# Two sequences per product in a fused linear-attention and channel-mix kernel

## The chip, the cores and the metric

The kernel runs on one core of a Trainium2 chip. A core has a matrix engine (TensorE, "PE" in the profile, its weight loads "PEld"), a vector engine (VectorE, "DVE"), a scalar engine (ScalarE, "ACT"), GpSimd ("POOL") and a queue engine (SyncE, "SP") that issues nearly all transfers. Work is done on 128 partitions; TensorE writes to PSUM, which has eight banks of 128 x 512 float32 numbers, and all else lies in SBUF or in device memory. The metric is the time on the device in microseconds.

## The reference

The input is `x`, 16 sequences of 1024 positions and 512 channels, float32. With 16 heads of 32 channels:

```python
qkv = x @ Wqkv.T + bqkv
q, k = rmsnorm(q, gq), rmsnorm(k, gk)
qf, kf = relu(rope(q)), relu(rope(k))
vk  = einsum('bhlp,bhld->bhpd', vpad, kf)      # vpad: v and a column of ones
res = einsum('bhpd,bhld->bhlp', vk, qf)
attn = res[..., :-1] / (res[..., -1:] + 1e-6)
x = layernorm(x + rmsnorm(attn @ Wout.T + bout, gout))
# then a channel mix with a shift by one position:
#   out = sigmoid(xr @ W_r.T) * (relu(xk @ W_k.T)**2 @ W_v.T)
x = layernorm(x + out)
```

Attention has no softmax, so all of a sequence's keys and values enter through one 32 x 32 matrix per head (`vk`) and one sum of keys per head.

## The kernel before

**Numbers in two parts.** A product keeps float32 precision by splitting each operand into a high part (rounded to the type float32r) and a low part (what is left). It is made as high x high + high x low + low x high. A split is a copy on ScalarE for the high part and a subtraction on VectorE for the low part.

**Tiles and slots.** `x` is cut into 128 tiles of 128 positions; tile `i` belongs to sequence `b = i // 8`. In the first stage, the function `slot(i)` takes tile `i`: it loads `x` both as it is (`xn`) and transposed (`xt`), projects `q` and `k` (`proj`, 12 products each of 512 columns), applies the rotation (`rope`), stores `q` in device memory for later, and adds to the sequence's `x^T k` (`add_kx`, 12 products into four PSUM banks of their own, `pskx`). GpSimd adds up the keys (`acc`). Values are never computed: since `v = x Wv^T + bv`, the matrix `v^T k` is `Wv (x^T k) + bv (sum of k)^T`.

**Closing a sequence.** In the slots after a sequence's last tile:

- `finish_a(b)` splits `x^T k` out of the four banks into high and low parts side by side (`kx`).
- `finish_s(b)` splits the key sums, adds them over the partitions with a product by ones (`psks`), copies the result to `ksv` and stores one row of it in device memory (`ks_d`).
- `finish_b(b)` makes `v^T k` for four groups of four heads (128 channels each). For each group and each of four chunks of the contraction it issues one product of 256 columns (high weight by the high and low parts of `kx`) and one of 128 columns (low weight by the high part). Two groups share one bank (`pskv`). VectorE adds the bias part, adds the two halves, masks out what lies between different heads and splits the result (`kvth`, `kvtl`).
- `finish_c(b, g)` multiplies group `g` by the output weight's rows for these heads (`w_o`, held in SBUF in two parts), splits it and stores it in device memory (`m_d`). One `finish_c` is done in each of four slots.

Later `load_m` reads that matrix back, and `part_q`, `part_qt`, `part_m`, `part_y` turn stored `q` tiles into the attention output, normalize it and add it to `x`. For the first 11 tiles, `part_q` comes in the first stage, one tile every 8 slots from slot 30; eight of them are carried through `part_y` there. After the last slot comes a transition in a fixed order, then the second stage: the channel mix in `NH` steps of four tiles, with the rest of the attention outputs between.

**Order of the work.** The first slots and the transition are in an order written out by hand. In between, the program gives each tile's work in the order of `slot`, and a planner then lays out each engine's queue from a simulated time line: it takes what is ready by its own costs, the earlier in the program first. Each engine runs its own queue strictly in order. `issue_after(load.ins)` only asks that a transfer stand behind that slot's `xt` load in SP's queue. Four PSUM banks are shared by all that is called `bank(...)` in the first stage: the seeds and products of `q` and `k`, and the closing work above. `late_load` and `late_split` bring in the weights of the later stages in set slots, one of four pieces at a time.

Of the kernel before, what the change touches and what calls it, by code (L numbers as in the profile page):

```python
# [15 lines left out]
P = 128  # L16
DIM = 512
# [5 lines left out]
NQ = 3  # L23
FIRST, STEP = 30, 8
NWARM = 8
HT = 512
# [7 lines left out]
def kernel(  # L34
# [275 lines left out]
    with ExitStack() as a_ctx:  # L310
# [41 lines left out]
        w_a = {h: tx.tile([P, NC_, DIM], F32R, name=f"wa_{h}") for h in "hl"}  # L352
        w_o = {h: te.tile([P, NC_, DIM], F32R, name=f"wout_{h}") for h in "hl"}

# [157 lines left out]

        fin, ksv = {}, {}

        def finish_a(b):

            kx = tx.tile([P, NC_, NC_, 2, P], F32R, tag="kx", name=f"kx{b}")
            for c, ps in enumerate(ps_kx.pop(b)):
                S.copy(kx[:, c, :, 0, :], groups(ps))
                V.tensor_sub(kx[:, c, :, 1, :], groups(ps), f32(kx[:, c, :, 0, :]))  # L520
            fin[b] = kx

        def split_keys(b):
            a = acc.pop(b)
            m = te.tile([P, 2, DIM], F32R, tag="m", bufs=2, name=f"ma{b}")
            S.copy(m[:, 0, :], a)
            V.tensor_sub(m[:, 1, :], a, f32(m[:, 0, :]))
            return m

        def finish_s(b, m=None):  # L530

            m = split_keys(b) if m is None else m
            ps = bank(f"psks{b}")
            for n in range(2):
                T.matmul(ps, lhsT=ones, rhs=m[:, n, :], start=(n == 0), stop=(n == 1))
            ksv[b] = tx.tile([P, DIM], F32, tag="ksv", name=f"ksv{b}")
            S.copy(ksv[b], ps)
            ks_d[b] = dram.tile([NC_, P], F32, name=f"ks_d{b}")
            nc.sync.dma_start(out=ks_d[b].rearrange("g p -> (g p)").unsqueeze(0), in_=ksv[b][0:1, :])

        def finish_b(b, places=(None, None)):

            kx, ks = fin.pop(b), ksv.pop(b)
            th = te.tile([P, NC_, P], F32R, tag="kvth", name=f"kvth{b}")
            tl = te.tile([P, NC_, P], F32R, tag="kvtl", name=f"kvtl{b}")
            for g in range(NC_):
# [21 lines left out]
                if g % 2 == 1:  # L568
                    two = slice(g - 1, g + 1)
                    kv = te.tile([P, 2, P], F32, tag="kv", bufs=1, name=f"kv{b}{g}")  # L570
# [11 lines left out]
                    V.tensor_mul(kv, kv, mask.unsqueeze(1).to_broadcast([P, 2, P]))  # L582
                    S.copy(th[:, two, :], kv)
                    V.tensor_sub(tl[:, two, :], kv, f32(th[:, two, :]))
            fin[b] = th, tl

        def finish_c(b, g, place=None):

            th, tl = fin[b]
            if g == 0:  # L590
                m_d[b] = dram.tile([P, 2, NC_, DIM], F32, name=f"m_d{b}")
            ps = bank(f"psm{b}{g}", place)
            for n, (a, r) in enumerate(((th, "h"), (th, "l"), (tl, "h"))):
                T.matmul(ps, lhsT=a[:, g, :], rhs=w_o[r][:, g, :], start=(n == 0), stop=(n == 2))
            m = te.tile([P, 2, DIM], F32R, tag="m", bufs=2, name=f"m{b}{g}")
            S.copy(m[:, 0, :], ps)
            V.tensor_sub(m[:, 1, :], ps, f32(m[:, 0, :]))
            nc.sync.dma_start(out=m_d[b][:, :, g, :], in_=f32(m))

        late = [("a", wqkv[:, :, 2 * DIM : 3 * DIM], c) for c in range(NC_)]  # L600
        late += [("o", wout, c) for c in range(NC_)]
        for n, w in (("k", wk), ("r", w_r), ("v", wv)):
            late += [(n, w, c) for c in range(NC_)]
            w_d[n] = dram.tile([P, NC_, 2, DIM], F32, name=f"w_d{n}")
# [9 lines left out]
        def late_split():  # L614
            _, n, c, st = staged.pop(0)
            if n in "ao":
                to = {"a": w_a, "o": w_o}[n]
                h, l = (to[k][:, c, :] for k in "hl")
            else:
                m = te.tile([P, 2, DIM], F32R, tag="m", bufs=2, name=f"w{n}{c}")  # L620
                h, l = m[:, 0, :], m[:, 1, :]
# [5 lines left out]
            V.tensor_sub(l, st, f32(h))  # L627
            if n not in "ao":
                nc.sync.dma_start(out=w_d[n][:, c, :, :], in_=f32(m))
# [161 lines left out]
        def late_step(i, load):  # L791
# [8 lines left out]

            if late and (3 <= i < 11 or i % 8 in (7, 0, 1) and not 23 <= i <= 26 and i > 14):
                with tc.issue_after(load.ins):
                    late_load(i)


        loads_m = {23 + c: (0, c) for c in range(NC_)}
        loads_m.update({n: (1, c) for c, n in enumerate((95, 96, 97, 103))})

        def slot(i):
# [12 lines left out]
            if b >= 0 and t == 7:  # L822
                finish_s(b)
            if i - 3 >= 0 and (i - 3) % 8 == 7:
                finish_b((i - 3) // 8)
            if i - 11 >= 0 and (i - 11) % 8 < NC_:
                finish_c((i - 11) // 8, (i - 11) % 8)
            add_kx(i - 1)
# [8 lines left out]
            if i + 2 < N:  # L837
                late_step(i, load)
            j, late_by = divmod(i - FIRST, STEP)
            if i in loads_m:  # L840
# [323 lines left out]
```

## Time and profile before

| | |
|---|---|
| median of 3 runs | 2708.42 us (2707.77 to 2710.29) |
| profiled execution | 2708.87 us, of which 2707.1 us is the span from first to last instruction |
| first stage | until about 1200 us |
| TensorE, share of the span | 99%, 12560 products and as many weight loads |
| VectorE, ScalarE, GpSimd | 80%, 70%, 26% |
| DMA | 433 MB, mean 160 GB/s |
| 300 to 900 us: VectorE, ScalarE, GpSimd busy | 483, 377, 140 of 600 us |
| 300 to 900 us: DMA busy share, rate | 0.76, 244 GB/s |
| one sequence of the first stage (8 slots) | 75.4 us |

In a line of the groups the columns are: line of the kernel, engine, operation, names written and read, shapes, count, then total busy time in us and mean length in ns, then the idle time of the engine just before them and what ended it. A line of the time line begins with start and length in us. Lengths of products overlap, since products are pipelined.

### The profile page before, as it was taken

How to read it: one execution, taken by the hardware profiler on the slowest of the kernel's cores; microseconds unless marked ns; L12 is line 12 of the kernel's file. 1: busy time of each engine (PE TensorE's matmuls, PEld its weight loads, DVE VectorE, ACT ScalarE, POOL GpSimd, SP SyncE). 2: the span in 40 equal slices, each digit the busy share in tenths (PEclk: the TensorE clock that was granted, in tenths of full speed). 3: DMA queues.
4: the chain of work that ended last, by engine and by line, in shares of the span. 5: the costliest groups of instructions: out<-in, count | busy, mean ns of one | idle time of the engine just before them, and what ended most of it. 6: DMA issues, size and time to landing. Idle time of an engine off the chain costs nothing.

```text
span 2707.1 us, 40178 instructions
## 1 busy us (share of the span) xinstructions
PE 2688.8 (99%) x12560; PEld 2230.7 (82%) x12560; DVE 2175.3 (80%) x4880; ACT 1883.2 (70%) x3820; POOL 695.6 (26%) x800
## 2 busy tenths in 40 slices
PE   9999999999999999999999999999999999999998
PEld 7888888888888888877888888888888888888887
DVE  8888888877888788776888888788888888888874
ACT  6666666666666556657777777777777777777775
POOL 4222222222222222234222222222222222222221
PEclk9999999999999999999999999999999999999999
DMA  7788888877777778754232332223133222313210
GB/s 248 241 262 267 259 266 260 264 233 232 228 230 231 251 248 255 247 199 145 90 117 63 105 98 86 88 92 117 59 109 94 87 92 92 113 59 111 73 58 33
DMA packets 232015, 433.29 MB, mean 160 GB/s; under 512 B 24676, under 2 KB 24932, under 8 KB 231800
## 3 DMA queue, kind: packets, MB, share of 16 engines
q1 hardware_dynamic: 231508, 430.19, 49.6%
q8 instruction: 99, 1.62, 0.2%
q14 instruction: 116, 0.95, 0.1%
q10 hardware_dynamic: 292, 0.53, 0.1%
HBM read 314.19 MB, written 116.42 MB: 159 GB/s over the span
## 4 chain that ended last, share of the span: by engine, by line
PE 51%; DVE 1%; ACT 0%; issue 0%; POOL 0%; POOLq 0%; ACTq 0%
PE psk L183 12%; PE psv L183 12%; PE psr L183 12%; PE psy L183 11%; PE pst L168 2%; PE psqt L168 2%; ACT x L288 0%; DVE mixr L901 0%; DVE q L240 0%; DVE mixk L901 0%; DVE gate L1042 0%; DVE mrl L917 0%; DVE qtl L252 0%; ACT gate L1030 0%; DVE den L237 0%
## 5 line engine op out<-in xcount | busy, mean ns | idle before, releaser
L183 PE MATMUL psk<-mkh,w_k 128*128 128x512 f32 x1024 | 332.7, 396 | 1.1 <-DVE kx L520 0.7
L183 PE MATMUL psv<-w_v,kah 128*128 128x512 f32 x1024 | 321.6, 395 | 0.6 <-DVE gate L1042 0.3
L183 PE MATMUL psy<-mb,qth 128*128 128x512 f32 x1024 | 320.0, 389 | 0.3 <-ACT qth L251 0.3
L183 PE MATMUL psr<-w_r,mrh 128*128 128x512 f32 x1024 | 318.6, 396 | 0.0
L183 PEld LDWEIGHTS psy<-mb,qth 128*128 128x128 f32 x1024 | 192.0, 188 | 40.5 <-ACT qth L251 0.7
L487 POOL TENSOR_TENSOR acc<-acc,ro 128x512 f32<-128x512 f32 x96 | 155.7, 1622 | 267.9 <-ACT ro L475 211.7
L183 PEld LDWEIGHTS psk<-mkh,w_k 128*128 128x128 f32 x1024 | 191.3, 188 | 40.3 <-DVE kx L520 1.0
L183 PEld LDWEIGHTS psr<-w_r,mrh 128*128 128x128 f32 x1024 | 188.7, 188 | 36.9 <-ACT r L952 0.2
L183 PEld LDWEIGHTS psv<-w_v,kah 128*128 128x128 f32 x1024 | 187.7, 188 | 38.0 <-DVE gate L1042 0.8
L147 POOL TENSOR_TENSOR rstd_all<-ss,mhalf 128x2 f32<-128x2 f32 x128 | 91.5, 715 | 473.8 <-DVE ss L470 459.5
L917 POOL TENSOR_TENSOR mkl<-mixk,mkh 128x512 fp32r<-128x512 f32 x127 | 165.7, 1305 | 182.4 <-ACT mkh L915 178.0
L429 PE MATMUL psq<-wqk_h,xh 128*128 128x512 f32 x512 | 200.5, 392 | 0.8 <-ACT wqk_h L667 0.8
L183 PE MATMUL psv<-w_v,kal 128*128 128x512 f32 x512 | 200.1, 391 | 0.0
L183 PE MATMUL psk<-mkl,w_k 128*128 128x512 f32 x512 | 199.8, 391 | 0.2 <-DVE mkl L917 0.2
L183 PE MATMUL psy<-mb,qtl 128*128 128x512 f32 x512 | 199.6, 390 | 0.0
L429 PE MATMUL psk<-wqk_h,xh 128*128 128x512 f32 x512 | 199.0, 390 | 0.2 <-ACT psk L360 0.2
L429 PE MATMUL psq<-wqk_l,xh 128*128 128x512 f32 x512 | 198.9, 389 | 0.0
L429 PE MATMUL psq<-wqk_h,xl 128*128 128x512 f32 x512 | 198.8, 389 | 0.0
L429 PE MATMUL psk<-wqk_h,xl 128*128 128x512 f32 x512 | 198.8, 389 | 0.0
L429 PE MATMUL psk<-wqk_l,xh 128*128 128x512 f32 x512 | 198.8, 389 | 0.0
L183 PE MATMUL psr<-w_r,mrl 128*128 128x512 f32 x512 | 196.5, 393 | 0.0
L147 POOL TENSOR_TENSOR yrs<-yss,mhalf 128x1 f32<-128x1 f32 x128 | 70.1, 548 | 395.0 <-DVE yss L300 297.7
(193 smaller groups left out, 7169.9 us busy)
## 6 DMA issues: line engine op xcount, KB each, us to landing
tab<-tab_d SPq DMA_DIRECT2D x480, 256.0 KB
xt<-in_xt_dram SPq DMA_DIRECT2D x128, 256.0 KB
xn<-in_x_dram SPq DMA_DIRECT2D x128, 256.0 KB
q_d<-ro SPq DMA_DIRECT2D x128, 256.0 KB
m_d<-m SPq DMA_DIRECT2D x64, 512.0 KB
mb<-m_d SPq DMA_DIRECT2D x64, 512.0 KB
q<-q_d SPq DMA_DIRECT2D x128, 256.0 KB
out_dram<-x SPq DMA_DIRECT2D x128, 256.0 KB
```

Source lines behind the costliest of these rows:

```text
L147: G.tensor_tensor(dst, src, mhalf[:, 0 : src.shape[1]], ALU.pow)
L168: T.matmul(ps[:, n * P : (n + 1) * P], lhsT=b, rhs=ident, is_transpose=True, start=(n == 0), stop=(n == NC_ - 1), skip_group_check=True,)
L183: T.matmul(ps, lhsT=a[u][:, rows], rhs=b[w][:, cols], start=(afresh and c == 0 and k == 0), stop=(c == n - 1 and k == 2), skip_group_check ...
L429: T.matmul(ps, lhsT=a[i][:, c, :], rhs=w_qk[b][:, c, cols], start=(not seeds and n == 0), stop=(seeds and n == 3 * NC_ - 1), skip_group_ch ...
L487: G.tensor_add(acc[b], acc[b], ros[i])
L917: (V if by_v else G).tensor_sub(ml, m, f32(mh))
```

## The change

Sequences 0 to 13 are taken in seven pairs; the last two stay as they were.

- `finish_a` of a paired sequence copies `x^T k` to SBUF in float32 (`kxf`, both sequences in one tile) and splits nothing.
- `split_kx(p, g)` splits one group of heads of both sequences. The two high parts and the two low parts lie side by side in the tile `stage`. It comes in slots u = 0, 2, 4, 6 of the pair, where u counts from slot 18 + 16 p.
- `finish_pair(p, g)` makes `v^T k` of one group for both sequences in slots u = 1, 3, 5, 7: for each chunk one product of 512 columns and one of 256 columns.
- `finish_c` of the two sequences comes in slots u = 2 to 9, one per slot.
- The key sums of a paired sequence are copied into a row of `acc` and stored; `load_ksv` reads those of both sequences back, on all partitions, half of the columns at a time (u = 0 and 4).
- The output weight is no longer held in SBUF. It is split and stored in device memory like the other late weights, and `load_wo` reads one group's rows into one of two buffers (u = 1, 3, 5, 7). For the last two sequences all four groups are loaded, two of them into the tile `stage` (`load_wo_last`).
- The slots in which later weights are loaded change, and so do those of the first sequence's `load_m` (28 to 31 instead of 23 to 26).

```diff
+PAIRS = 7
-        w_o = {h: te.tile([P, NC_, DIM], F32R, name=f"wout_{h}") for h in "hl"}
...
         def finish_a(b):
+            if paired(b):
+                p, s = divmod(b, 2)
+                if s == 0:
+                    kxf[p] = tx.tile([P, 2, NC_, DIM], F32, tag="kx", name=f"kxf{p}")
+                for c, ps in enumerate(ps_kx.pop(b)):
+                    S.copy(kxf[p][:, s, c, :], ps)
+                return
...
+            if paired(b):
+                row = acc.pop(b)[0:1, :]
+                S.copy(row, ps[0:1, :])
...
+        def load_ksv(p, half):
+            ksv[p, half] = tx.tile([P, 2, 2 * P], F32, tag="ksv", name=f"ksv{p}{half}")
+            cols = slice(half * 2 * P, (half + 1) * 2 * P)
+            nc.sync.dma_start(
+                out=ksv[p, half],
+                in_=ks_p[p].rearrange("s g n -> s (g n)")[:, cols].partition_broadcast(P),
+            )
+        def load_wo(g):
+            w_o[g] = te.tile([P, 2, DIM], F32R, tag="wo", bufs=2, name=f"wo{g}")
+            nc.sync.dma_start(out=f32(w_o[g]), in_=w_d["o"][:, g, :, :])
...
+        def split_kx(p, g):
+            st = te.tile([P, NC_, 2, 2, P], F32R, tag="stage", name=f"kx{p}{g}")
+            for s in range(2):
+                a = kxf[p][:, s, :, g * P : (g + 1) * P]
+                S.copy(st[:, :, s, 0, :], a)
+                V.tensor_sub(st[:, :, s, 1, :], a, f32(st[:, :, s, 0, :]))
+            staged_kx[p] = st
...
+        def finish_pair(p, g):
+            st = staged_kx.pop(p)
+            cols = slice(g * P, (g + 1) * P)
+            ps = bank(f"pskv{p}{g}")
+            four = ps.rearrange("p (s two n) -> p s two n", s=2, two=2)
+            for c in range(NC_):
+                T.matmul(ps, lhsT=w_a["h"][:, c, cols],
+                    rhs=st[:, c].rearrange("p s two n -> p (s two n)"), ...)
+                T.matmul(four[:, :, 0, :], lhsT=w_a["l"][:, c, cols],
+                    rhs=st[:, c, :, 0, :], ...)
+            kv = te.tile([P, 2, P], F32, tag="kv", bufs=1, name=f"kv{p}{g}")
+            V.scalar_tensor_tensor(kv,
+                ksv[p, g // 2][:, :, g % 2 * P : (g % 2 + 1) * P],
+                bv[:, g : g + 1], four[:, :, 0, :], ALU.mult, ALU.add)
+            V.tensor_add(kv, kv, four[:, :, 1, :])
+            V.tensor_mul(kv, kv, mask.unsqueeze(1).to_broadcast([P, 2, P]))
+            th, tl = parts(p, g)
+            S.copy(th, kv)
+            V.tensor_sub(tl, kv, f32(th))
...
-            if late and (3 <= i < 11 or i % 8 in (7, 0, 1) and not 23 <= i <= 26 and i > 14):
+            if late and (3 <= i < 11 or i % 16 > 10 and not 27 <= i < 32):
...
-        loads_m = {23 + c: (0, c) for c in range(NC_)}
+        loads_m = {28 + c: (0, c) for c in range(NC_)}
...
-            if i - 3 >= 0 and (i - 3) % 8 == 7:
-                finish_b((i - 3) // 8)
-            if i - 11 >= 0 and (i - 11) % 8 < NC_:
-                finish_c((i - 11) // 8, (i - 11) % 8)
+            p, u = divmod(i - 18, 16)
+            if 0 <= p < PAIRS and u in (0, 2, 4, 6):
+                split_kx(p, u // 2)
+            if 0 <= p < PAIRS and u in (1, 3, 5, 7):
+                finish_pair(p, u // 2)
+            if 0 <= p < PAIRS and 2 <= u < 10:
+                finish_c(2 * p + u % 2, u // 2 - 1)
+            if i == 8 * 2 * PAIRS + 10:
+                finish_b(2 * PAIRS)
+            if 0 <= i - 8 * 2 * PAIRS - 11 < NC_:
+                finish_c(2 * PAIRS, i - 8 * 2 * PAIRS - 11)
...
+            if 0 <= p < PAIRS and u in (0, 1, 3, 4, 5, 7):
+                with tc.issue_after(load.ins):
+                    if u % 4 == 0:
+                        load_ksv(p, u // 4)
+                    else:
+                        load_wo(u // 2)
+            u = i - 8 * 2 * PAIRS - 9
+            if 0 <= u < NC_:
+                with tc.issue_after(load.ins):
+                    (load_wo, load_wo_last)[u % 2]((0, 2, 1, 3)[u])
```

## The prediction

> **What bounds the kernel now.** I read the busy shares first, then the chain that ended last, then TensorE's waits, then the groups of the edited lines, then the time line around one of them. Page, parts 1, 2 and 4:
>
> ```profile
> span 2707.1 us, 40178 instructions
> PE 2688.8 (99%) x12560; PEld 2230.7 (82%) x12560; DVE 2175.3 (80%) x4880; ACT 1883.2 (70%) x3820; POOL 695.6 (26%) x800
> ...
> PEclk9999999999999999999999999999999999999999
> ...
> PE 51%; DVE 1%; ACT 0%; issue 0%; POOL 0%; POOLq 0%; ACTq 0%
> ```
>
> TensorE is never idle and never throttled. Its waits between 100 and 1000 us are none, and between 1000 and 1200 us one of 0.5 us (for `kh`). So the first stage, which the change rewrites, lasts as long as TensorE's instructions do: time taken out of them comes off the end, unless another engine's lateness takes their place.
>
> What an instruction costs is the distance between starts, not the listed length (a busy TensorE is modelled). Time line of TensorE, columns start and length:
>
> ```profile
> 180.61 0.34 PE L552 MATMUL pskv<-kx,wa_h 128*128 128x256 f32 x1
> 180.78 0.23 PE L560 MATMUL pskv<-kx,wa_l 128*128 128x128 f32 x1
> 180.84 0.33 PE L552 MATMUL pskv<-kx,wa_h 128*128 128x256 f32 x1
> ...
> 184.37 0.39 PE L429 MATMUL psq<-wqk_h,xh 128*128 128x512 f32 x1
> 184.59 0.39 PE L429 MATMUL psq<-wqk_l,xh 128*128 128x512 f32 x1
> 184.82 0.39 PE L429 MATMUL psq<-wqk_h,xl 128*128 128x512 f32 x1
> ```
>
> A 512-column step is 0.226 us. A 256-column product and the 128-column one after it take 0.231 together (180.61 to 180.84), though they stream fewer columns than one 512: two weight loads set that, 0.115 each. The transposes, 128 columns each, step at 0.109, the same limit.
>
> **The change part by part.**
>
> *Products.* Per sequence `finish_b` issues 16 pairs of 256 and 128 columns: 16 x 0.231 = 3.70 us, 7.39 for two sequences. `finish_pair` does two in 16 pairs of 512 and 256 columns. The 512 step is 0.226. The trace has no run of 256-column steps under such a partner. Bounds: 0.109 (transpose step, weight load alone) to 0.171 (the longest distance that follows a 256-column start, 180.61 to 180.78). I take 0.115, half the pair above, since half a 512 step is 0.113 too. Then 16 x 0.341 = 5.46; saved 1.93 per pair of sequences, 13.5 us for seven pairs; by the bounds 14.2 and 7.3. The skill's "TensorE: Matmul & The Clock Gate", sections "Back-to-back issue gap" and "LDWEIGHTS", gives columns/2.4 + 2.5 ns and 128/1.2 = 107 ns per load. By it the old pair is 216 ns, the new one 325, and the saving 112 x 107 ns = 12.0. The rows say 231 and 226 where it says 216 and 216, so I use the rows.
>
> *Copies.* For 14 sequences `finish_a` now only copies four banks to float32 on ScalarE (4 x 0.598, row of L519); `split_kx` then copies and subtracts from SBUF, 8 of each per pair. ScalarE gains 56 copies x 0.62 = 35 us, beside a busy share of 59 to 66% in this stage. VectorE's 56 subtractions move from a PSUM source to an SBUF source. Rows:
>
> ```profile
> L520 DVE TENSOR_TENSOR kx<-pskx,kx 128x512 fp32r<-128x512 f32 x64 | 39.8, 681 | 2.4 <-ACT kx L519 2.3
> L348 DVE TENSOR_TENSOR xnl<-xn,xnh 128x512 fp32r<-128x512 f32 x128 | 94.3, 736 | 43.9 <-ACT xnh L347 43.9
> L476 DVE TENSOR_TENSOR kl<-ro,kh 128x512 fp32r<-128x512 f32 x128 | 108.1, 845 | 62.4 <-ACT ro L475 62.4
> ```
>
> From PSUM 681 ns, from SBUF 736 or 845. The skill's "SBUF — State Buffer", section "Who interferes with whom", speaks against this move: a VectorE instruction with two SBUF inputs blocks against a GpSimd instruction that reads SBUF, for all of it. This trace agrees: a `kl` of 1.49 us at 479.35 beside GpSimd's `acc` sum at 479.01 (1.28 us). By the `xnl` row the move costs 56 x 0.055 = 3 us of VectorE; by the rule up to a whole `acc` sum each, 56 x 1.62 = 91, or 13 per pair. GpSimd is busy 23% of the stage and a hit lasts half a sum on average: 0.23 x 0.8 x 56 = 10, or 1.5 per pair, an estimate. I take that. Against it `finish_pair` has four half-width scalar products fewer per pair, 8 x 0.34 against 4 x about 0.45 (between 0.34 and 0.68; nearest the 256-wide rows of 0.41 to 0.44): 0.9 per pair back.
>
> The PSUM banks of `pskx` come free after the copies alone; four subtractions no longer stand before the next sequence's first `add_kx`. TensorE did not wait there, so nothing for this.
>
> *DMA.* Per pair four `load_wo` of 512 KB and two `load_ksv` of 256 KB, all on SP's queue: 2.6 MB in eight slots of about 9.4 us, beside 244 GB/s at a busy share of 0.76 (full rate 320 GB/s by division). That is 35 GB/s more: about 0.87 while it lasts; six issues of 0.32 to 0.5 us per 75 us of SP. Each `wo` half-buffer is freed two slots before its load and read one slot after: hidden. The `ksv` halves land a slot ahead of VectorE: hidden. At the end (slots 121 to 124) a `wo` buffer is freed in the same slot as its reload; a late one holds SP's `xt` and table loads behind it and costs one wait of at most 3 us, which I put at 0.3. The output weight's four stores (512 KB) fall in the first 100 us, as its splits do already; the later weight loads only change slots. The first sequence's `mb` loads move from slots 23 to 26 to slots 28 to 31, the last one slot ahead of its product, with one load a slot as before. If that slot (over 8 us) did not cover the landing (5.6 us from issue to use for `q`), TensorE would wait once, by a few us. I put nothing for these. The sum row is now copied into `acc`, so GpSimd's first `acc` sum waits for that row's store. Before, `ksv` was copied at 468.60 and the sum began at 479.01: 10 us for a 2 KB store; nothing.
>
> *Crowding.* This is what could cost. Before, nearly every slot had one piece of side work; now slots u=0 to 7 of each sixteen have the pair's work too, and u=5, 6, 7 coincide with `part_q`, `part_m`/`part_y` and `finish_a`. VectorE per slot by rows: 6.56 base (`xl`, `xnl`, two ropes, `kl`); split 1.4; pair 1.97; `finish_c` 0.68; `part_q` with `part_qt` 3.6; `part_y` 2.4; `finish_a` 2.7; sums 0.73. The rows' ends overlap: eight slots sum to 69 by them, but the windows show 62.1 and 62.6 of 75.4 us busy, so x 0.89. Densest four slots before (i mod 8 = 7, 0, 1, 2): 40.0 x 0.89 + 3.5 wait for `q` = 39.1, against TensorE's 39.9. After (u = 4 to 7): 42.5 x 0.89 + 3.5 = 41.3 against 41.7. The slack falls from 0.8 to 0.4. How near that is to a stall:
>
> ```profile
> 429.08 0.79 DVE L233 SCALAR_TENSOR_TENSOR pr<-q,ksb 128x512 f32<-128x512 f32 x1 [3.55 <-DMA q<-q_d]
> ...
> 431.25 0.69 DVE L476 TENSOR_TENSOR kl<-ro,kh 128x512 fp32r<-128x512 f32 x1
> ```
>
> `kl` ends at 431.94 and TensorE starts the product that reads it at 433.02: 1.1 us of margin behind a 3.55 us wait for `q`. In other slots this margin is down to 0.05 us (between 940 and 1060 us). So I allow 0.15 us a pair, 1.0 in all.
>
> **Sum.** Span 2707.1, of a profiled execution of 2708.87: -13.5 + 1.0 + 0.3 = -12.2, giving 2694.9 and 2696.7. That execution lies 0.4 us above the median of the runs, 2708.42; from the median 2696.2. I predict 2696.2, faster by 0.45%. A difference under 0.2% (5.4 us) could not be told from none.
>
> **Rivals.** *A: `q` lands late and takes back the gain.* In u=4 `q` shares the queue with half a `ksv` (256 KB) and comes after a `wo` (512 KB): at 320 GB/s 0.8 and 1.6 us more, 2.4 less the margin of 1.1 = 1.3 a pair, 9 us. Time 2704 to 2706, about no change. For: all eleven `part_q` of this stage waited, 37.4 us together. Against: only every second `q` falls in u=4, and it was asked for 5.6 us before.
>
> *B: VectorE becomes the bound in u=0 to 7; slower.* Place: `kl`, or the seeds of `psq`, which wait for a bank that VectorE reads last: five banks' worth of tiles (`psq`, `psk`, `pskv`, `psm`, `psqt` or `psks`) pass through four in u=5 and 7, where four was the most before. For: the `psq` seed after `finish_b` ended at 482.06 with its product at 482.81. Against: `pskv` now holds a bank for 8 products, not 16. If port blocking is nearer the rule (5 us a pair in place of 1.5), the 0.4 slack becomes a lag of 3 us: seven times 3 is 21, time 2717. From a stall of 1.9 us a pair (13.5 / 7) nothing is left of the gain; beyond it the kernel is slower.
>
> *C: the 256 step stays at 0.171.* Saved 7.3: 2702. Against: weight loads alone never step slower than 0.115 in this trace.
>
> **Chances and range.** Forecast (2692 to 2700) 0.60; C and partial stalls (2700 to 2703) 0.10; A and what else ends near no change (2703 to 2714) 0.14; B (over 2714) 0.16. Faster by over 0.2% (under 2703) is the first two, 0.70; same 0.14; slower 0.16. The range for 8 in 10 takes in the first two and most of A and leaves out B: 2692 to 2710.
>
> **What would show it.** Right: products of `finish_pair` at 0.34 per pair of starts; TensorE's instructions 224 fewer each of products and loads; its waits still near none up to 1000 us; the start of the last sequence's products some 13 us earlier. Wrong: waits of TensorE for `kl`, `psq` seeds or `pskv`, once per sixteen slots; `kx` subtractions well over 0.74; the wait of `pr` for `q` over 3.6. A wrong sum would come from the order that the planner writes for each engine, which the edits redraw throughout the stage and which this trace can't show.

## The result and the profile after

The changed kernel takes 2741.66 us, the median of 4 runs (2739.19 to 2743.21); the kernel before takes 2708.1 us beside it. The ratio is 1.0122 with a 95% interval of 1.0105 to 1.014: slower by 1.2%, 33.6 us. The forecast was 2696.2. The profiled execution took 2739.19 us and its span is 2737.4 us, 30.3 us longer than before.

From the page of the changed kernel, parts 1 and 4:

```profile
span 2737.4 us, 39858 instructions
...
PE 2689.9 (98%) x12336; PEld 2214.0 (81%) x12336; DVE 2197.7 (80%) x4852; ACT 1909.8 (70%) x3876; POOL 696.0 (25%) x800
...
PE 61%; DVE 3%; DMA 1%; ACT 1%; issue 1%; POOL 0%; POOLq 0%; SPq 0%; DVEq 0%; ACTq 0%
```

TensorE has 224 products fewer, as the forecast said. Yet the span is longer, and the chain that ended last now goes through VectorE for 3% and ScalarE for 1%, where it had 1% and 0% before. The whole loss lies in the first stage. The second key-sum product of the last sequence starts at 1207.4 us before and at 1237.9 after, 30.5 later; what comes behind it takes the same time in both.

The windows of the changed kernel, by stretches of 100 us; the columns are busy us and instructions of TensorE, its loads, VectorE, ScalarE and GpSimd, then the granted clock, the DMA share and GB/s:

```profile
200.00:300.00 100.00, 100.00 (x448) 82.89 (x447) 80.85 (x141) 62.79 (x133) 23.85 (x21) 1.00 0.85 279
300.00:400.00 100.00, 94.66 (x412) 76.95 (x411) 76.36 (x144) 62.80 (x132) 20.54 (x21) 0.97 0.72 229
...
900.00:1000.00 100.00, 95.99 (x425) 77.79 (x424) 82.19 (x142) 58.55 (x127) 22.78 (x21) 1.00 0.85 271
1000.00:1100.00 100.00, 100.00 (x446) 82.91 (x445) 82.57 (x139) 66.28 (x140) 22.61 (x21) 1.00 0.79 252
```

TensorE is full between 200 and 300 us, where the first pair is closed, and from 1000 us on. Between 300 and 1000 it is not. VectorE is no busier where TensorE starves (76 and 82 of 100 us) than where it doesn't (81 and 83).

TensorE's waits of the changed kernel between 100 and 1230 us (us in total, times, longest):

```profile
PE psq L429 <- ACT psq L163: 14.5, 10, 2.0
PE pskx L505 <- ACT kh L474: 6.9, 7, 2.1
PE pskx L505 <- DVE kl L476: 3.9, 6, 1.4
PE psk L429 <- ACT psk L163: 3.8, 3, 1.8
PE psm L691 <- DVE m L694: 1.3, 1, 1.3
```

The largest is the product of `q` that waits for its seed, the copy of the bias into a bank by ScalarE (L163). Before, the same view had no line above 0.8 us.

**Where the 30 us are.** I measured the distance between the starts of consecutive products. What a distance over 0.33 us has above the usual step (0.2265 us for 512 columns, 0.1155 below) is called a stall here. Distances of 0.39 to 0.44 us are counted apart, as slow steps. Take the 64 slots from tile 34 to tile 98, the four pairs that meet both `part_q` and `part_y`:

| tiles 34 to 98 | before | after |
|---|---|---|
| length | 600.4 | 634.8 |
| stalls | 0.5 | 34.5 |
| slow steps | 0 | 5.9 (30 of them) |

Stalls and slow steps add 39.9; the products save 7.7 by the forecast's 1.93 a pair; the other 2.2 of the 34.4 are small delays below the bound. By sixteen slots, from tile 18 on, the lengths before were 150.3, 150.8, 150.8, 150.8, 147.9 and 143.5; after they are 148.1, 160.5, 159.7, 158.8, 155.8 and 146.8. The first pair, whose closing ends before any `q` work begins, is 2.2 us **shorter**. Each of the next four is 8 to 10 us longer. The sixth of the row (pair 5), which still meets a `part_q` but no `part_y`, is 3.3 longer. What lies before tile 18 and after tile 114 is 4.9 shorter together (the closing of the first sequence goes out of the one and part of a pair's comes into the other), which leaves the 30.5.

The stalls come at the same places of each sixteen slots (u as in the change, counted here by the tile whose products of `q` and `k` are under way). Of 40.5 us between 100 and 1230, 17.4 lie at u = 4, in five pairs, and 9.1 at u = 8, nearly all of it in four. `part_q` is written at u = 5 of pairs 1 to 5 and `part_y` at u = 6 of pairs 1 to 4: five and four.

**The stall at u = 8.** Time line of the changed kernel around 394.6 us; columns start, length, engine:

```profile
390.21 0.69 DVE L298 TENSOR_TENSOR y<-psy,g_out 128x512 f32<-128x512 f32 x1 [2.05 <-PE psy L184]
...
390.93 0.60 ACT L300 ACTIVATE junky<-psy 128x512 bf16<-128x512 f32 x1 [2.87 <-DVE y L298]
...
393.51 0.72 ACT L283 ACTIVATE junka<-x,nma 128x512 bf16<-128x512 f32 x1 [1.89 <-DVE nma L281]
...
394.60 0.40 PE L691 MATMUL psm<-wo,kvtl 128*128 128x512 f32 x1
...
396.31 0.60 ACT L163 COPY psq<-b_qk 128x512 f32<-128x512 f32 x1
396.50 0.68 DVE L461 TENSOR_TENSOR t<-psq,tab 128x512 f32<-128x512 f32 x1
...
396.96 0.51 PE L429 MATMUL psq<-wqk_h,xh 128*128 128x512 f32 x1 [1.96 <-ACT psq L163]
```

TensorE issues its last product at 394.60 and its next one only at 396.96, when the seed of 396.31 has landed. That seed stands in ScalarE's queue behind `junka`, a step of `part_y`'s layer norm, and behind four more instructions (2.1 us), two of them the pair's. ScalarE came to a stop twice for that chain, 2.87 us for VectorE's `y` and 1.89 for `nma`, while VectorE itself had stopped 2.05 us for the product `psy`. Three engines waited for each other, each with other work behind the waiting instruction. The stall is 2.13 us at 394.60, at 556.72, at 714.56 and 2.12 at 874.71.

The first of the two stops is not new. ScalarE in the kernel before:

```profile
391.42 0.60 ACT L299 ACTIVATE junky<-psy 128x512 bf16<-128x512 f32 x1 [2.84 <-DVE y L297]
...
392.14 0.59 ACT L162 COPY psq<-b_qk 128x512 f32<-128x512 f32 x1
...
394.85 0.72 ACT L282 ACTIVATE junka<-x,nma 128x512 bf16<-128x512 f32 x1
```

There it stopped 21.5 us for `y` in the eight tiles (17.8 after), and TensorE lost nothing: each time the seed of `psq` stands directly behind `junky`, and `junka`, behind the seed, waits for nothing. In the changed kernel the seed is still ahead of `junka` for four of the eight tiles, and these have no such stall. In the other four `junka` stands ahead of the seed with its wait of 1.89 us, and these are the four stalls.

**The stall at u = 4.** The same view around 668.6 us:

```profile
664.60 1.29 POOL L487 TENSOR_TENSOR acc<-acc,ro 128x512 f32<-128x512 f32 x1 [4.00 <-ACT ro L475]
...
665.14 1.29 DVE L234 SCALAR_TENSOR_TENSOR pr<-q,ksb 128x512 f32<-128x512 f32 x1 [1.34 <-DMA q<-q_d]
...
667.81 0.68 DVE L461 TENSOR_TENSOR t<-psq,tab 128x512 f32<-128x512 f32 x1
...
669.86 0.59 ACT L163 COPY psq<-b_qk 128x512 f32<-128x512 f32 x1 [3.72 <-DVE ro L463]
...
670.50 0.51 PE L429 MATMUL psq<-wqk_h,xh 128*128 128x512 f32 x1 [1.49 <-ACT psq L163]
```

`pr`, the first step of `part_q`, waits for `q` at the head of VectorE's queue and then runs beside GpSimd's sum. The rotation that reads the bank of `psq` (667.81) stands behind it, so that bank comes free at 669.83 and its new seed starts at 669.86; ScalarE had stopped 3.72 us for it. The other banks are held too: `pskv` of this slot, whose products start at 663.73, is read by VectorE at 672.35 for the first time and at 675.14 for the last, 12 us in all. TensorE loses 1.66 us here and 2.16 more at 673.11, where `kh` is late in ScalarE's queue.

The lines of the groups that answer to those shown before, changed kernel:

```profile
L589 DVE TENSOR_TENSOR kx<-kxf,kx 128x512 fp32r<-128x512 f32 x56 | 37.5, 681 | 3.0 <-ACT kx L588 3.0
L476 DVE TENSOR_TENSOR kl<-ro,kh 128x512 fp32r<-128x512 f32 x128 | 115.3, 901 | 37.4 <-ACT ro L475 36.6
L635 DVE TENSOR_TENSOR kvtl<-kv,kvth 128x256 fp32r<-128x256 f32 x28 | 25.9, 926 | 0.0
L623 DVE SCALAR_TENSOR_TENSOR kv<-ksv,bv,pskv 128x256 f32<-128x256 f32 x28 | 13.2, 471 | 1.8 <-PE pskv L614 1.8
```

And the products of `finish_pair` on TensorE's time line:

```profile
392.27 0.39 PE L606 MATMUL pskv<-kx,wa_h 128*128 128x512 f32 x1
392.50 0.28 PE L614 MATMUL pskv<-kx,wa_l 128*128 128x256 f32 x1
392.61 0.40 PE L606 MATMUL pskv<-kx,wa_h 128*128 128x512 f32 x1
```

Two starts of the wide product lie 0.34 us apart here, 0.351 by the medians of all (0.233 and 0.118).

### The profile page after: what moved, and what is told of

Same layout as the page of the kernel before. It is cut to its first block, busy times and chain, and to the rows that moved or that the text cites. A ratio compares the mean times of both kernels' runs of the same rounds, so it can differ in the third digit from the quotient of the medians.

```text
span 2737.4 us, 39858 instructions
## 1 busy us (share of the span) xinstructions
PE 2689.9 (98%) x12336; PEld 2214.0 (81%) x12336; DVE 2197.7 (80%) x4852; ACT 1909.8 (70%) x3876; POOL 696.0 (25%) x800
## 4 chain that ended last, share of the span: by engine, by line
PE 61%; DVE 3%; DMA 1%; ACT 1%; issue 1%; POOL 0%; POOLq 0%; SPq 0%; DVEq 0%; ACTq 0%
PE psr L184 13%; PE psk L184 12%; PE psv L184 12%; PE psy L184 12%; PE psk L429 3%; PE pskx L505 3%; PE psq L429 3%; PE pst L169 2%; PE psqt L169 2%; PE psm L691 1%; DMA xn<-in_x_dram 0%; DVE t L461 0%; DMA xt<-in_xt_dram 0%; DVE ro L463 0%; DMA q<-q_d 0%
## 5 line engine op out<-in xcount | busy, mean ns | idle before, releaser
L429 PE MATMUL psq<-wqk_h,xh 128*128 128x512 f32 x512 | 202.7, 396 | 15.4 <-ACT psq L163 14.5
L474 ACT ACTIVATE kh<-ro,rstd_all 128x512 fp32r<-128x512 f32 x128 | 92.9, 726 | 115.3 <-DVE ro L463 96.5
```

Of the source, the lines that this page charges most:

```text
L429: T.matmul(ps, lhsT=a[i][:, c, :], rhs=w_qk[b][:, c, cols], start=(not seeds and n == 0), stop=(seeds and n == 3 * NC_ - 1), skip_group_ch ...
L474: S.activation(kh, r, AF.Relu, scale=rstd_all[:, i, 1:2])
```

## The experiments

**What could do it.** My theory after the traces: the order of the queues. The pair's closing and the `q` work of every eighth tile meet in the same slots, and whatever waits at the head of VectorE's and ScalarE's queues (`pr` for its load, `y` for its product, the chain of the layer norm over three engines) delays the release of the four shared banks and the seeds behind it (O in the expectations). The rivals: the added transfers (D), the added work of VectorE or its port blocking (V), the number of tiles that pass through the four banks and how long each is held (K), and the place of the `q` work alone. Every kernel below is the changed kernel with the edit shown; ratios are to the kernel before, run beside it.

**q34: the `q` work four slots later** (u = 1, 2, 9, 10 in place of 5, 6, 13, 14).

```diff
-FIRST, STEP = 30, 8
+FIRST, STEP = 34, 8
```

> One number changed: FIRST 34 in place of 30, so part_q falls on u=1 and 9 and part_y on u=2 and 10 of a pair's sixteen slots, instead of u=5, 13 and 6, 14. Theory V (VectorE's queue is too long in the slots where q work and pair work meet): TensorE's stalls between 300 and 1000 us (35 us) fall to under 10, time 2700 to 2712. Theory K (pskv and psm hold two of the four shared banks at once): the same place is relieved, since psqt and psy then meet one closing bank and not two; also 2700 to 2712. Theory D (the reloads of wo and ksv delay the tables, xn and q): nothing changes, over 2730.

Measured: 2730.16 us, ratio 1.0079 (1.0064 to 1.0095). Stalls 34.4, now spread over u = 0 to 4 and 8 (5.2, 3.4, 2.8, 2.4, 8.4, 7.0). Shifting the meeting within the closing moves the stalls and takes back 11 us of 33.

**noload: the added transfers left out.** Only the first of each buffer is loaded, so 26 of 28 `wo` and 13 of 14 `ksv` loads are gone and the later groups use the rows loaded first.

```diff
         def load_wo(g):
+            if len(wos) == 2:
+                w_o[g] = wos[g % 2]
+                return
...
+            wos[g] = w_o[g]
...
         def load_ksv(p, half):
+            if ksvs:
+                ksv[p, half] = ksvs[0]
+                return
...
+            ksvs[0] = ksv[p, half]
...
```

> The changed kernel without 26 of 28 paired loads of wo and without 13 of 14 loads of ksv: the first ones' data is used again, so the output weight's rows and the key sums are the wrong ones, while every product, copy and subtraction stays. 17 MB of transfers are gone. Theory D: VectorE's waits for tab and xn go and with them most stalls; time 2700 to 2712. Theories V and K: within 5 us of the changed kernel, 2735 to 2745.

Measured: 2732.87 us, 1.0094 (1.0079 to 1.0109). Stalls 36.2, of which 14.0 at u = 4 and 8.9 at u = 8. The transfers are worth some 8 us, mostly at u = 3 and 4 (21.5 us of stalls in the changed kernel, 15.4 here), where `pr` waits for `q` in the same queue. Most of the loss stays.

**gsub: the subtractions of `split_kx` on GpSimd.**

```diff
-                V.tensor_sub(st[:, :, s, 1, :], a, f32(st[:, :, s, 0, :]))
+                G.tensor_sub(st[:, :, s, 1, :], a, f32(st[:, :, s, 0, :]))
```

> split_kx's subtractions on GpSimd in place of VectorE: VectorE does 1.36 us less in each of u=0, 2, 4, 6, GpSimd some 2.7 more. Theory V: the stalls fall by half or more, 2705 to 2722, unless GpSimd's own lateness (rstd_all behind the subtractions) takes their place. Theories K and D: 2735 to 2745.

Measured: 2742.85 us, 1.0131 (1.0116 to 1.0146); stalls 42.8. The windows' sum from 300 to 1000 us, kernel before:

```profile
sum 700.00, PE 699.89 PEld 583.55 DVE 563.70 ACT 438.99 POOL 163.33; mean PE 699.89 PEld 583.55 DVE 563.70 ACT 438.99 POOL 163.33
```

The changed kernel:

```profile
sum 700.00, PE 670.39 PEld 543.51 DVE 555.06 ACT 430.47 POOL 153.91; mean PE 670.39 PEld 543.51 DVE 555.06 ACT 430.47 POOL 153.91
```

This kernel:

```profile
sum 700.00, PE 672.39 PEld 543.79 DVE 543.47 ACT 432.09 POOL 201.79; mean PE 672.39 PEld 543.79 DVE 543.47 ACT 432.09 POOL 201.79
```

The slower kernels get through less work in these 700 us, so compare the same 64 slots too, tiles 34 to 98: VectorE is busy 483.9 of 600.4 us before, 502.8 of 634.8 after and 490.1 of 635.1 here. In the slots u = 4 to 7 of these pairs it is 117.0 of 148.0 us before, 147.1 of 188.5 after and 137.0 of 181.5 here. VectorE does have more to do where the pair's work is, but with 12 us taken off it nothing is gained, and more than a fifth of its time there is idle. It stands still with work behind it. This run does not take the port blocking away, since GpSimd now reads SBUF for longer (201.8 us in place of 153.9).

**acopy: ScalarE copies `pskv` out of its bank**, so that the bank no longer waits for VectorE's two reads.

```diff
-            kv = te.tile([P, 2, P], F32, tag="kv", bufs=1, name=f"kv{p}{g}")
+            pc = te.tile([P, 2, 2, P], F32, tag="kv", bufs=1, name=f"kv{p}{g}")
+            S.copy(pc, four)
+            four = pc
+            kv = pc[:, :, 0, :]
...
```

> ScalarE copies pskv out of PSUM right after finish_pair's products and VectorE reads the copy: the bank is held for about 2 us in place of 8 (median), VectorE's count of instructions stays, ScalarE does 0.6 us more in four slots. Theory K: stalls fall by half or more, 2705 to 2722. Theory V: VectorE is as late as before, 2735 to 2750. Theory D: 2738 to 2745.

Measured: 2729.65 us, 1.0088 (1.0071 to 1.0105). Stalls 29.4: u = 4 falls from 17.4 to 6.9, u = 8 goes from 9.1 to 11.0. How long `pskv` keeps its bank matters at u = 4 and not at u = 8.

**noq: `q` work of tiles 1, 3, 5 and 7 left out of the first stage** (their attention output is never made). These are the tiles that meet pairs 1 to 4 at u = 5 and 6; tile 9, whose `part_q` meets pair 5, stays.

```diff
-                if late_by == 1:
+                odd = j % 2 == 1 and j < NPRE
+                if late_by == 1 and not odd:
                     part_q(j)
...
-                    part_s(j)
-                    part_y(j, part_m(j))
+                    if odd:
+                        qs.pop(j)
+                    else:
+                        part_s(j)
+                        part_y(j, part_m(j))
```

> The changed kernel with the q work of tiles 1, 3, 5 and 7 left out of the first stage (loads stay; part_q, part_qt, part_m and part_y of these four are not done, so their outputs are wrong): in the pairs' slots u=4 to 6 there is no q work any more, but for tile 9's part_q. TensorE has 64 products of 0.11 to 0.23 us less, 12.6 us. If the stalls come from pair work and q work in the same slots, the large ones at u=3, 4 and 8 of pairs 1 to 4 vanish (24 of 40 us and the slow steps after them): 2698 to 2706. If pair work alone makes them: 2741 - 12.6 = 2729.

Measured: 2697.08 us, 0.996 (0.9945 to 0.9975). What is left out is 12 products and four transposes for each tile, 4 x (12 x 0.2265 + 4 x 0.109) = 12.6 us of TensorE, so the time compares to 2709.7. Stalls 18.0 in place of 40.5. Waits of TensorE from 300 to 1000 us:

```profile
PE pskx L505 <- ACT kh L474: 4.1, 5, 2.1
PE psq L429 <- ACT psq L163: 2.0, 2, 1.5
```

At u = 8 there is nothing left. At u = 4, tile 102 has its two stalls as before (1.65 and 2.27), and tiles 38, 54, 70 and 86 together 1.7 us: the stall stays where a `part_q` still meets the closing and goes where it doesn't. The pair's work alone does not make these stalls. But 2709.7 is no more than level with before: the 13.5 us that the products should save don't come through even so.

**nopsm: the products of `finish_c` of the odd sequences left out** (a constant is stored in their place). It takes every second `psm` tile out of the four banks, and 19.0 us of TensorE.

```diff
+            if paired(b) and b % 2 == 1:
+                m = te.tile([P, 2, DIM], F32R, tag="m", bufs=2, name=f"m{b}{g}")
+                S.copy(m[:, 0, :], b_out)
...
+                return
             ps = bank(f"psm{b}{g}", place)
```

> The changed kernel with finish_c's three products of the odd sequence of each pair left out (m is made from b_out, so that sequence's matrix is wrong); the copy, the subtraction and the store stay. TensorE does 84 products less, 19.0 us, and half of the psm banks are not taken. Theory K (banks): stalls fall by half or more, 2741 - 19 - 17 = 2705 or less. Theory O (what stands in front in the in-order queues of VectorE and ScalarE while they wait for each other): stalls stay, 2718 to 2725.

Measured: 2726.84 us, 1.0072 (1.0057 to 1.0087). With the 19.0 put back that is 2745.8, and stalls are 46.1. Stalls at u = 4 fall from 17.4 to 3.7, but those at u = 3 grow from 4.1 to 7.3, at u = 8 from 9.1 to 13.3 and at u = 12 to 15 from 6.5 to 17.1. Fewer tiles in the banks do not help in all, so their number is not the whole cause; its share at u = 4 stays open, since these slots are also 0.68 us of TensorE shorter and the queues are drawn anew.

**shorty: `part_y` of tiles 1, 3, 5 and 7 cut to two VectorE instructions** (no sum of squares, no normalization).

```diff
+                    ps = part_m(j)
+                    if j % 2 == 1:
+                        y = tp.tile([P, DIM], F32, tag="y", bufs=2, name=f"y{j}")
+                        V.tensor_mul(y, ps, g_out)
+                        V.tensor_add(xs[j], y, xs[j])
+                    else:
+                        part_y(j, ps)
```

> The changed kernel with part_y of tiles 1, 3, 5 and 7 cut to y = ps * g and x + y (no norms, so these outputs are wrong): the chain of part_y that passes from VectorE to ScalarE, GpSimd and back is gone in u=6 to 8; banks and products stay. Theory O: the stall of 2.1 us at u=8, where the seed of psq stands on ScalarE behind that chain's second square, vanishes (4 x 2.1 us and what follows): 2725 to 2733. Theory K: within 5 us of 2741.

Measured: 2724.15 us, 1.0069 (1.0052 to 1.0086). Stalls 29.4: u = 8 falls from 9.1 to nothing, u = 4 stays at 17.8. Waits of TensorE, 300 to 1000 us:

```profile
PE pskx L505 <- ACT kh L474: 6.1, 3, 2.1
PE psq L429 <- ACT psq L163: 6.0, 6, 1.5
PE psk L429 <- ACT psk L163: 3.5, 2, 1.8
```

The stall at u = 8 is `part_y`'s chain. TensorE's work is the same here as in the changed kernel; ScalarE and VectorE have less, so `spread`, which keeps all work, is the cleaner proof.

**spread: the layer norm of `part_y` one slot later in the program**, all work kept.

```diff
-                    part_y(j, part_m(j))
+                    ysteps[j] = part_y_steps(j, part_m(j))
+                    next(ysteps[j])
+                    next(ysteps[j])
+                if late_by == 3 and j < NPRE:
+                    for _ in ysteps.pop(j):
+                        pass
...
```

> The changed kernel with one edit: the layer norm at the end of part_y is traced one slot later than part_y's first steps, so the planner ranks it behind the next slot's copies and seeds. Theory O (order in the in-order queues): the stall of 2.1 us at u=8 shrinks as in acspread (to about 1.2) and the smaller ones after it; the stalls at u=4 stay: 2720 to 2730. If the gain of acspread over acopy needs the early release of pskv: 2735 to 2742.

Measured: 2728.73 us, 1.0074 (1.0057 to 1.0091). Stalls 35.4: u = 8 falls to 5.8, four times 1.34 us; u = 4 stays at 17.3.

**acspread: acopy and spread together.**

> ScalarE copies pskv out of PSUM (as in the run acopy), and part_y's layer norm is traced one slot later than its first steps, so that the planner ranks it behind the next slot's seeds. Theory O with K: the stalls at u=8 (11.0 us in acopy) go, 2715 to 2722. Theory K alone: as acopy, 2727 to 2732.

Measured: 2708.84 us over 12 runs, 1.0008 (0.9999 to 1.0016). Stalls 18.8 (u = 4 6.0, u = 8 5.3), and no slow step. Waits of TensorE, 300 to 1000 us:

```profile
PE psq L429 <- ACT psq L163: 7.8, 9, 1.5
PE pskx L505 <- DVE kl L476: 0.6, 2, 0.3
```

Two edits that take away no work, and even add 28 copies to ScalarE, give back nearly all of the loss, 33 us. Alone they gave 12 and 13. Sixteen slots are now 150.7, 152.8, 151.4 and 148.8 us for pairs 1 to 4, in all 3.4 us more than before, so the gain of the products is still being spent on what is left of the stalls.

**prorder: `part_q`'s first VectorE instruction held behind the `kl` of its slot.**

```diff
                 if late_by == 1:
+                    dve = mybir.EngineType.DVE
+                    before, n = last_of(dve), len(nc.cur_bb.bb.instructions)
                     part_q(j)
+                    not_before(next(k for k in nc.cur_bb.bb.instructions[n:] if k.engine == dve), before)
```

> The changed kernel with one edit: the first instruction of part_q on VectorE may not stand before the newest instruction that the same slot traced there (kl of tile i). VectorE's wait for q (24.7 us in nine places) goes, since q has long landed by then. Theory O: the stalls at u=3 and 4 (21 us with TensorE's waits for kl and the seed of psq behind them) fall by half or more: 2715 to 2727. If u=4 is a matter of VectorE's load or of banks: 2736 to 2745.

Measured: 2758.16 us, 1.0184 (1.0169 to 1.0199). Stalls 53.5: u = 3 and 4 fall from 21.5 to 0.8, but u = 14 has 21.1, u = 8 12.8 and u = 6 8.1. VectorE's waits in this kernel, 300 to 1000 us:

```profile
DVE xnl L349 <- ACT xnh L348: 35.3, 21, 3.2
DVE y L298 <- PE psy L184: 34.4, 8, 8.4
```

The stall at u = 4 belongs to `pr`'s place in the queue. But `q` now comes so late that the products of `part_m` are late too, and VectorE waits 34 us at the head of its queue for eight `psy` (9.1 in the changed kernel). The wait has moved, and grown.

**acdefer: acopy, and all of `part_y` one slot later, between two rotations.**

```diff
                 rope(i, j, qk[j])
+                if j == 0 and pending:
+                    k, ps = pending.pop()
+                    part_y(k, ps)
...
-                    part_y(j, part_m(j))
+                    pending.append((j, part_m(j)))
```

> acopy, and the whole of part_y after its products traced one slot later, between the next slot's two ropes: y, which waits for psy, may then stand behind t of psq on VectorE. Theory O: the u=8 stall (1.2 us in acspread) goes; 2700 to 2707. Against it: psy holds its bank for some us longer; if banks decide, 2710 to 2725.

Measured: 2714.37 us, 1.0028 (1.0016 to 1.004). Stalls 25.0: none at u = 8, 7.2 at u = 4, and 6.8 at u = 12, where there were 1.6.

**acdeferpr: acdefer with prorder.**

> acdefer and prorder together. Theory O: no large stall is left, 2694 to 2700, which is the gain that the products alone make. If the order of part_q makes VectorE late elsewhere: over 2705.

Measured: 2734.94 us, 1.01 (1.0085 to 1.0115). Stalls 36.6, 21.6 of them at u = 14. The imposed place of `pr` does the same harm here.

**prshift: prorder, with `part_qt` one slot behind `part_q` and `part_m`, `part_y` one slot behind that** (each one slot later than it was), so that `q`'s lateness meets no one.

```diff
-                    if j <= NPRE:
-                        part_qt(j)
-                if late_by == 2 and j < NPRE:
+                if late_by == 2 and j <= NPRE:
+                    part_qt(j)
+                if late_by == 3 and j < NPRE:
                     part_s(j)
```

> prorder with part_qt one slot later than part_q and part_m with part_y one slot later again, so that the transposes no longer wait for a part_q that stands late in its own slot. Theory O: the stalls at u=3 and 4 stay away, as in prorder (0.8 us), and prorder's new ones (21 us at u=14, 8 at u=6, TensorE waiting for q and kh behind it) go too; the part_y stall moves one slot on and stays (8 to 13 us): 2712 to 2725. If every place that the q work is given makes stalls of its own (the slots are simply too full): 2735 to 2755.

Measured: 2727.22 us, 1.0072 (1.0057 to 1.0087). Stalls 31.0: u = 14 is mended, u = 4 has 2.8, and `part_y`'s chain shows a slot later, at u = 9, with 15.5.

**best: prshift with acopy and spread.**

> prshift with the early release of pskv (acopy) and the later layer norm (spread). Theory O: 2696 to 2704. If the slots are too full: over 2709.

Measured: 2712.51 us over 20 runs, 1.0018 (1.0011 to 1.0025). Stalls 18.8: none at u = 4, 8.2 at u = 9 (four times), 4.9 at u = 15. It is 15 us better than prshift and no better than acspread: mending u = 4 altogether brought the stall elsewhere.

**acsprshift: acspread with the later slots of prshift, but no imposed order.**

> acspread with part_qt and the rest of the q work one slot later, and no order imposed on part_q. Tells whether the gain of the run best, if there is one, comes from the later slots or from part_q's place on VectorE. If from part_q's place: the stalls at u=4 (6.0 us in acspread) stay, 2705 to 2712. If from the slots: as best.

Measured: 2726.56 us, 1.0071 (1.0055 to 1.0088). Stalls 29.4, at u = 0 (8.5), 9 (8.3) and 15 (7.0), 0.7 at u = 4. Later slots by themselves cost acspread 18 us.

**qlate: no `q` work in u = 0 to 8**, by a list of start slots in place of every eighth.

```diff
-FIRST, STEP = 30, 8
+START = (31, 44, 47, 60, 63, 76, 79, 92, 95, 108, 111)
...
-            j, late_by = divmod(i - FIRST, STEP)
+            j = sum(i >= n for n in START) - 1
+            late_by = i - START[j]
...
```

> The changed kernel with only the slots of the q work moved: tiles start in slots 31, 44, 47, 60, 63, 76, 79, 92, 95, 108, 111 in place of 30, 38, 46 and so on, so part_q falls on u=11 and 14 and part_y on u=12 and 15, and no q work is left in the pairs' slots u=0 to 8. If the meeting of pair work and q work is what costs, the stalls at u=3, 4 and 8 (31 us) go and the rest stays about 10: 2698 to 2708. If two q tiles three slots apart crowd in the same way: 2715 to 2740.

Measured: 2723.15 us, 1.0055 (1.0042 to 1.0067). Stalls 29.0. At u = 3, 4 and 8 only 1.7 of 30.6 us is left, with all work kept: here the meeting of the two kinds of work is what stalled TensorE. But the time misses its forecast, for u = 15, where the copies of `finish_a` now meet `q` work, has 12.9 us, more than half of it right after `psks`, and TensorE's first wait is now `pskx` for the copies `kxf` (6.7 us in 4).

**qlateac: qlate, with acopy and spread.**

> qlate with the early release of pskv (acopy) and the layer norm one slot later (spread). If the two edits that helped before add to qlate: 2694 to 2700, faster than both kernels. If qlate leaves nothing for them: as qlate.

Measured: 2702.3 us over 14 runs (2701.27 to 2703.79), 0.998 (0.9972 to 0.9988). Stalls 12.8, slow steps 0.4. Waits of TensorE, 300 to 1000 us:

```profile
PE pskx L505 <- ACT kxf L525: 1.4, 2, 1.0
PE psq L429 <- ACT psq L163: 0.4, 1, 0.4
...
```

This one beats both kernels: the one before by 0.2%, the changed one by 1.4%. The second key-sum product of the last sequence starts at 1200.5, 6.9 us earlier than before. About half of the products' gain comes through. The same edits were not tried on the kernel before; it has 6.0 us of stalls in the stage to lose.

**What is shown and what is not.** Shown: the stalls at u = 3, 4 and 8 need the closing of a pair and `q` work in the same slots (noq, qlate); the part at u = 8 is `part_y`'s chain (shorty, spread, and the order of `junka` and the seed); it is not VectorE's load (gsub), not the number of tiles in the banks alone (nopsm), and some 8 us of it are the transfers (noload); and edits that only change where an instruction stands or how soon a bank is let go move the time by 33 us down (acspread) or 16.5 up (prorder). Open: the share of each place, and what port blocking and held banks add at u = 4. Every edit lets the planner draw all queues anew, so the parts don't add (12 and 13 alone, 33 together), and how full a slot is can't be varied without the order. What is left of the gain between 2702 and the forecast was not followed up.

## Why the prediction was wrong

**Products: right.** A pair of a wide and a narrow product takes 0.351 us where the forecast took 0.341, so the half-step taken for 256 columns (0.115) was near (0.118) and rival C's 0.171 was not seen. The first pair, which meets nothing, is 2.2 us shorter; 1.93 was forecast.

**Copies: the blocking was undersized, and fell on others.** `kx` from SBUF took 681 ns, as from PSUM, where 736 and 10 us of blocking in all were allowed. The rule of the skill's "SBUF — State Buffer", "Who interferes with whom", showed in other instructions: between 300 and 1000 us the mean of `xnl` went from 686 to 806 ns, of `kl` from 812 to 857, of `kvtl` from 478 to 843 and of `pr` from 875 to 1068, and all 34 of these that were clearly stretched ran beside an `acc` sum. By the means that is 20 us in 700, or about 4.5 in a pair's 159 us (an estimate), where 1.5 was allowed. The scalar products of 256 columns took 471 ns (about 450 forecast). ScalarE's copies fit in. gsub takes as much as 12 us off VectorE in the same stretch for nothing, so the size of its work is not what counts; what the blocking alone costs no run shows.

**DMA, late weights, the `acc` row: hidden, nearly.** The wait of `pr` for `q` is 24.7 us in 9 between 300 and 1000 us, against 29.8 in 9 before, the longest 3.7 against 3.9. Rival A, `q` landing later, did not happen. Without the added loads the kernel gains some 8 us, which the forecast had as nothing.

**Crowding: the step that failed.** It said the slack of the densest four slots falls from 0.8 to 0.4 us and allowed 0.15 us a pair, 1.0 in all. Measured: four pairs got 8 to 10 us longer and a fifth 3.3, 38 us in all, although each should have saved 1.93; so the cost is 10 to 12 us a pair in four of them. The step added busy times, and one wait for `q`, over four slots of VectorE and compared the sum with TensorE's. Such a sum sees a wait only as so many us on one engine. It doesn't see that the waiting instruction holds what stands behind it, that the held one keeps a bank, that the bank keeps a seed on a second engine, and that engine's next work waits as well. VectorE had a fifth of the stage idle, and of the slots u = 4 to 7 as well, and still came late. The traces of before gave the figure that mattered: a margin of 1.1 us behind a wait of 3.55, and of 0.05 us in other slots. ScalarE's stop of 2.84 us for `y` was there before as well and cost nothing; what cost 2.1 us in each of four pairs was a further stop, of 1.89 us, that the new order put in front of a seed. The forecast said in its last sentence that the planner's order could make it wrong and gave that no share of its own.

**Rival B: the right place, the mechanism right in part at most.** The seeds of `psq` that wait, once per sixteen slots, were named, with the point from which the kernel is slower (1.9 us a pair) and a chance of 0.16. The blocking that it assumed, 5 us a pair, nearly came, but VectorE as the bound fell with gsub, and more tiles than banks as the whole cause with nopsm. Its size, 3 us a pair, was too low by more than half, for it had one stall a pair and there were three, with slow steps after some.

## What to carry to other kernels

Where engines run their queues in order and a few banks pass between them, ask of each instruction that can wait how long it waits and what stands behind it, on its own engine and then on the next; a sum of busy times over some slots can't show a stall. Work that saves time on the bound engine but doubles up in slots which already hold a chain over three engines should be judged by the margin of those slots, not the mean, against the chain's waits. A wait that costs nothing can start to cost when one seed changes places with it. What helped here was to let banks go early (a copy on an engine with time to spare) and to write the steps of the chain further apart; together they gave more than the sum of both, and holding one instruction back by force, alone, made things worse.

## What was not expected of the hardware

TensorE's clock was halved after short stalls. Time line of the changed kernel after the stalls of 1.53 and 1.66 us that end at 350.56, then its windows before, in and behind the slow stretch (the granted clock is the third number from the end):

```profile
350.56 0.79 PE L429 MATMUL psq<-wqk_h,xh 128*128 128x512 f32 x1 [1.50 <-ACT psq L163]
351.15 0.63 PE L429 MATMUL psq<-wqk_l,xh 128*128 128x512 f32 x1
351.57 0.63 PE L429 MATMUL psq<-wqk_h,xl 128*128 128x512 f32 x1
```

```profile
346.89:350.30 3.41, 1.19 (x4) 0.67 (x4) 3.41 (x9) 0.39 (x1) 0.00 (x0) 1.00 0.51 183
350.30:353.72 3.42, 3.17 (x8) 2.49 (x9) 3.42 (x8) 2.27 (x5) 0.70 (x1) 0.50 0.85 271
353.72:357.13 3.41, 2.90 (x13) 2.08 (x12) 3.29 (x7) 2.36 (x6) 0.37 (x1) 1.00 0.85 299
```

Steps are 0.427 us in place of 0.2265 for six products, then normal again. It happened four times, with 6 to 8 slow steps each. Other stalls of the same 2 us (556.7, 714.6 and 874.7) have none. The trace's clock records tell why: the clock is at 0.50 from 350.30, 398.09, 517.55 and 835.00, for 3.413 us each, and these times lie 14, 35 and 93 times 3.413 us apart. So the clock is set on a fixed grid, and what counts is how much of one grid stretch is idle: 73, 66, 59 and 60% of the stretch before each fall (idle taken as the distance between starts less the usual step), while the other stalls lie across two stretches, and no other stretch reaches 56%. In the traces of all 19 kernels, between 100 and 1230 us, all 43 stretches at full clock with 60% or more idle were followed by half clock, and none of the 6171 with less than 58%; in between it was six of seven. The skill's "TensorE: Matmul & The Clock Gate", "What's actually happening", puts the fall of the clock at an idle window of about 3.4 us; the length agrees, but the window need not be idle throughout, for here no single distance was over 2.6 us. In all it is 5.9 us, so a stall can cost more than its length, and whether it does depends on where it falls on the grid.
